# The last image's closing chain: reciprocals spread by products, a convolution started in chunks, depthwise steps shared between two engines, and products that nothing reads

## The chip, the cores and the metric

The kernel runs on one core of a Trainium2 chip. Its time is the device time of one execution in microseconds (us); three executions took 3289.28, 3290.07 and 3290.38 us. The engines are called PE (matrix products), DVE (vector), ACT (activations), POOL and SP (here mostly the queue that starts transfers). All tensors are 32-bit floats.

## The reference, cut to what matters

Eight images x of 512 channels and 64x64 pixels pass two layers, each with a residual connection and a group normalisation of 32 groups in front. The first is a deformable attention with 8 heads; the second is a narrow bottleneck.

```python
x = x + attention(group_norm(x))      # ends: softmax(q k) v, divided by the sum of exps, then w_out
x = x + bottleneck(group_norm(x))

def bottleneck(x):
    y = conv1x1(x, conv_w, conv_b)            # 512 channels to 32, all 4096 pixels
    y = depthwise_conv(y, dw_w, dw_b)         # 3x3, stride 2: 64x64 to 32x32
    y = fc1(y); y = fc2(y)                    # 1024 to 256 to 1024, per channel
    y = depthwise_deconv(y, de_w, de_b)       # 3x3: 32x32 to 64x64
    return conv1x1(y, out_w, out_b)           # 32 channels to 512
```

The group normalisation of the second layer needs mean and variance over all pixels of an image. So the bottleneck of an image can't begin its scaling before the attention of that image has ended.

## The kernel before, in words

The pixels of an image are cut into 8 tiles of 512 (`NT`, `TP`), the channels into 4 blocks of 128 (`NCC`, `P`). Heads go in pairs, so a round of the main loop is one (image, tile, pair of heads), 32 rounds to an image and 256 in all. The order is written out by hand; each engine works through its list in that order. In a round:

- `logits` makes the products of queries and keys and their exponentials for the next round, and `weighted_values` the products with the values (`pa`).
- `sum_exps` adds up the exponentials by products with a selecting matrix into `pn`. After the fourth pair of a tile `invert` takes the reciprocal `rn` on DVE and moves two rows of it to each other half by four small transfers on SP. `scale_two` then spreads one row over 32 partitions (`stream_shuffle`) and multiplies it onto the pair's result, one pair at a time.
- `project_out`, six rounds later (`LAG`), makes one block of `w_out` times the result: eight products of 64 columns each into `pp`. DVE adds bias and residual, and takes statistics (`bn_stats`). The residual itself was read from memory by `load_residual`, over the place that the tile's queries had held.

The bottleneck of image b is `layer1`, a generator. For seven images its pieces lie between the rounds of the next image. For the last image there is no next image: the loop runs `LAG` rounds more without logits, and then `layer1_last` is drained in one go. Its steps, each waiting for the one before: `group_stats` (aggregates on DVE, a product for the group means, small operations on DVE, a product for the variances, a power of -1/2 on POOL); the scaled weights `cw`; the convolution `py`, 32 products of 32 columns; its copy into `y` on ACT, the bias, and three copies of rows that border on another part; nine depthwise steps on DVE into `z`; two transposes `pz` and a copy; the two matrices of the perceptron (`ph`, `pht`, `pu`) with copies between; the deconvolution (`upsample`, four calls for row halves h and parities a, nine DVE operations per h); and `project_last`, 32 products of 32 rows (`out_product`), each evicted with the residual added by DVE (24 of them), or by ACT and then POOL (8 of them, tiles 4 and 5), and each written to memory by a transfer of 256 KB on SP. Transfers on SP stand in the order of the code, so one that isn't ready holds those behind it.

The PSUM pools `ps_s` (two pairs of banks), `ps_a` (`pa` and `pn`) and `ps_mm` (two banks) are shared by all these products. `wflat` is one buffer that holds `y`, `z`, its transpose, `u` and the result `v` of the deconvolution.

Of the kernel before, what the change touches and what calls it, by code (L numbers as in the profile page):

```python
# [49 lines left out]
def kernel(  # L50
# [53 lines left out]
    def q_tile(b, t):  # L104
        return spot(b, t)
# [555 lines left out]
    def project_out(b, t, oc, st):  # L661

        ao, xt = q_tile(b, t), out_tile(b, t)
        pp = ps_mm.tile([P, TP], F32, tag="mm", name=f"pp_{b}_{t}_{oc}")
        for hp in range(NCC):
            for r in (0, DH):
                nc.tensor.matmul(  # L667
                    pp[r : r + DH, :],
                    wout[:, hp, oc * P + r : oc * P + r + DH],
                    ao[:, hp, :],  # L670
                    start=(hp == 0),
                    stop=(hp == NCC - 1),
                )
        nc.vector.scalar_tensor_tensor(  # L674
            xt[:, oc, :], pp, col(V_BOUT + oc), xt[:, oc, :], ALU.add, ALU.add
        )
        nc.vector.bn_stats(st[:, oc, t, :], xt[:, oc, :])  # L677
# [50 lines left out]


    def layer1(b, st, project, place, v):  # L730
# [10 lines left out]
        gs = yield from group_stats(st, 1, b)  # L741
        cw = small.tile([P, NCC, CB], F32, tag="cw", name=f"cw_{b}")
        nc.vector.tensor_mul(cw, convw, gs[:, 1].unsqueeze(2).to_broadcast([P, NCC, CB]))
        yield None

        py = [ps_mm.tile([P, TP], F32, tag="mm", name=f"py_{b}_{h}") for h in range(2)]
        for h in range(2):
            for cc in range(NCC):
                for rb in range(4):
                    nc.tensor.matmul(  # L750
                        py[h][rb * CB : (rb + 1) * CB, :],
                        cw[:, cc, :],
                        out_tile(b, 2 * rb + h)[:, cc, :],
                        start=(cc == 0),
                        stop=(cc == NCC - 1),
                    )

        y = wflat[:, : (ROWS + 1) * (HW + 1)].rearrange("p (r c) -> p r c", c=HW + 1)
        nc.vector.memset(y[:, :, 0:1], 0.0)
        nc.vector.memset(y[0:CB, 0:1, :], 0.0)  # L760
        for h in range(2):
            nc.scalar.copy(
                y[:, 1 + 8 * h : 9 + 8 * h, 1:], py[h].rearrange("p (r c) -> p r c", c=HW)
            )
        pb = ps_mm.tile([P, TP], F32, tag="mm", name=f"pb_{b}")
        for cc in range(NCC):
            for rb in range(4):
                nc.tensor.matmul(
                    pb[rb * CB : (rb + 1) * CB, 0:1],
                    cw[:, cc, :],  # L770
                    gs[:, 0, cc : cc + 1],
                    start=(cc == 0),
                    stop=(cc == NCC - 1),
                )
        yb = small.tile([P, 1], F32, tag="yb", name=f"yb_{b}")
        nc.vector.tensor_sub(yb, col(V_CONVB), pb[:, 0:1])
        nc.vector.tensor_scalar_add(y[:, 1:, 1:], y[:, 1:, 1:], yb)
# [11 lines left out]
        z3 = z.rearrange("p (i j) -> p i j", j=32)  # L789
        for k in range(9):  # L790
            ki, kj = divmod(k, 3)
            yk = y[:, ki : ki + 15 : 2, kj : kj + 63 : 2]
            w = col(V_DWW + k)
            if k == 0:
                nc.vector.tensor_scalar(z3, yk, w, col(V_DWB), ALU.mult, ALU.add)
            else:
                nc.vector.scalar_tensor_tensor(z3, yk, w, z3, ALU.mult, ALU.add)
# [4 lines left out]
        for h in range(2):  # L802
            nc.tensor.transpose(pz[:, h * P : (h + 1) * P], z[:, h * P : (h + 1) * P], ident)
        o += NK
# [6 lines left out]
        for k in range(8):  # L811
            rb, h = divmod(k, 2)
            j = k % 4
            nc.tensor.matmul(
                ph[j * CB : (j + 1) * CB, : 2 * P],
                zT[:, h, rb * CB : (rb + 1) * CB],
                w1[:, k, :],
                start=(k < 4),
                stop=(k >= 4),
            )  # L820
        parts4 = z
# [5 lines left out]
        for oc in range(2):  # L827
# [6 lines left out]
            )  # L834
        hT = small.tile([P, 2, CB], F32, tag="hT", name=f"hT_{b}")
# [8 lines left out]
        for n0, n, rbs in ((0, NK, 4), (NK, 32, 3)):  # L844
            for oc in range(2):
                for rb in range(rbs):
# [7 lines left out]
                    )  # L854

# [28 lines left out]

        for h, a in ((0, 0), (0, 1), (1, 0)):
            upsample(h, a)
            yield None
# [100 lines left out]
    def layer1_last(b, st, other):  # L988
        return layer1(b, st, project_last(other), spot(other, 0), wbuf[:, 0:2, :])
# [69 lines left out]
    with tc.manual_schedule():  # L1059
# [38 lines left out]
        for g in range(len(names) + LAG):  # L1098
# [12 lines left out]
            summed = g % 2 == 0 and 0 <= g - 1 < len(names)  # L1111
            if g % 2 == 0:
                scale_two()
            if g < len(names):
                weighted_values(*names[g])
            if summed:
                sum_exps(*names[g - 1])
            if g < len(names):
                add_exps(*names[g])
# [24 lines left out]
            if 0 <= k < len(names) and k % NCC < 2:  # L1144
                load_residual(*names[k + k % NCC], 2)
# [11 lines left out]
        drain(layer1_last(B - 1, st1s.pop(B - 1), B - 2))  # L1157
# [118 lines left out]
```

## Time and profile before

| | |
|---|---|
| median of the three runs | 3290.07 us (3289.28 to 3290.38) |
| profiled execution, own time | 3290.23 us |
| its span in the profile | 3288.5 us |
| PE busy over the span | 3207.7 us, 98% |
| DVE, ACT, POOL busy | 2330.8, 1186.2, 612.2 us |
| granted PE clock, mean | 0.99 of full speed |
| moved by transfers | 390.62 MB |

The profiled execution lasted 1.7 us longer than its span. The span is cut into 40 slices of 82 us in the page's second part. PE is busy in tenths at 9 in all slices but the first and the last, and the last slice shows PE at 6, the granted clock at 6, and transfers at 125 GB/s. That slice is the closing chain of the last image, and a finer look at it is the way to read this case. A matrix product's entry counts its two passes as two instructions; its end is modelled, so neighbouring products overlap by some hundredths of a microsecond.

### The profile page before, as it was taken

Reading aid. Unit: us, or ns where it says so; the run is one execution under the profiler, and the core shown is the slowest. Engines: PE = TensorE matmul, PEld = TensorE weight load, DVE = VectorE, ACT = ScalarE, POOL = GpSimd, SP = SyncE. Lnnn points to the kernel's source line nnn. Section 1 sums busy time; section 2 is a strip of 40 time slices with the busy share of each in tenths; the row PEclk is TensorE's granted clock in tenths of the full one; section 3 lists DMA queues with packets and bytes.
Section 4 is the critical chain, followed back from the end, with each engine's and each line's share of the span. In section 5 each row is a group of like instructions: output and inputs, shape, how many; then the busy total and the mean of one; then the engine's idle time right before and its main releaser. Section 6 shows DMA issues by size and latency. Waiting matters only on the chain.

```text
span 3288.5 us, 46198 instructions
## 1 busy us (share of the span) xinstructions
PE 3207.7 (98%) x18196; PEld 1531.2 (47%) x18196; DVE 2330.8 (71%) x3786; ACT 1186.2 (36%) x1641; POOL 612.2 (19%) x576
## 2 busy tenths in 40 slices
PE   6999999999999999999999999999999999999996
PEld 5884223348332583326733276332853338433222
DVE  7884765787757777587765977668776687757564
ACT  2343333343333433344333443324433344333520
POOL 1130300130402304022030221303021040310201
PEclk9999999999999999999999999999999999999996
DMA  7232222672327623284333843248232482322713
GB/s 275 77 93 76 76 78 65 198 156 75 113 91 213 126 86 103 78 235 115 104 100 103 209 100 111 83 160 194 71 104 89 181 180 65 121 73 77 130 44 125
DMA packets 293874, 390.62 MB, mean 119 GB/s; under 512 B 18320, under 2 KB 157840, under 8 KB 293648
## 3 DMA queue, kind: packets, MB, share of 16 engines
q1 hardware_dynamic: 240368, 261.72, 24.4%
q0 software_dynamic: 53280, 125.86, 17.1%
q8 instruction: 145, 2.38, 0.3%
q14 instruction: 81, 0.66, 0.1%
HBM read 193.52 MB, written 192.94 MB: 118 GB/s over the span
## 4 chain that ended last, share of the span: by engine, by line
PE 94%; DVE 4%; issue 1%; ACT 0%; DMA 0%; SPq 0%; POOL 0%; ACTq 0%; DVEq 0%; POOLq 0%
PE pp L667 27%; PE pq L275 23%; PE ps L580 14%; PE pa L598 13%; PE pn L625 4%; PE pqt L324 4%; PE pk L533 2%; PE py L750 2%; PE pv L560 2%; PE po L893 2%; DVE rn L638 1%; PE po L424 0%; PE pu L848 0%; DVE st L201 0%; PE po_s L893 0%
## 5 line engine op out<-in xcount | busy, mean ns | idle before, releaser
L667 PE MATMUL pp<-image,wout 128*64 128x512 f32 x3584 | 821.3, 600 | 3.6 <-DVE image L653 3.4
L588 ACT ACTIVATE es<-ps 128x1024 f32<-128x1024 f32 x512 | 504.0, 1022 | 274.0 <-PE ps L580 211.1
L667 PEld LDWEIGHTS pp<-image,wout 128*64 128x64 f32 x3584 | 237.3, 137 | 549.5 <-issue 474.6
L598 PE MATMUL pa<-es,vt 128*64 128x512 f32 x2048 | 488.9, 598 | 1.7 <-ACT es L588 1.7
L275 PE MATMUL pq<-image,wbuf 128*128 128x256 f32 x2048 | 476.3, 381 | 3.3 <-DVE image L217 1.9
L519 POOL DMA_INDIRECT g<-qd,row x256 | 280.4, 1095 | 1056.2 <-DVE row L516 990.0
L580 PE MATMUL ps<-image,kt 64*64 64x512 f32 x3584 | 437.3, 602 | 0.3
L275 PEld LDWEIGHTS pq<-image,wbuf 128*128 128x128 f32 x2048 | 381.8, 191 | 56.0 <-issue 5.0
L674 DVE SCALAR_TENSOR_TENSOR image<-pp,vec,image 128x512 f32<-128x512 f32 x224 | 167.2, 746 | 337.8 <-PE pp L667 334.2
L605 ACT COPY image<-pa 128x512 f32<-128x512 f32 x224 | 131.9, 589 | 658.9 <-PE pa L598 650.5
L610 DVE TENSOR_TENSOR es<-es,es 128x1024 f32<-128x1024 f32 x256 | 310.9, 1215 | 71.4 <-PE pa L598 71.4
L598 PEld LDWEIGHTS pa<-es,vt 128*64 128x64 f32 x2048 | 137.3, 137 | 294.5 <-issue 274.1
L580 PEld LDWEIGHTS ps<-image,kt 64*64 64x64 f32 x3584 | 114.4, 132 | 307.4 <-issue 182.0
L638 DVE RECIPROCAL rn<-pn 128x512 f32<-128x512 f32 x64 | 214.6, 3353 | 7.7 <-PE pn L625 5.8
L334 ACT COPY qr<-pqt 128x512 f32<-128x512 f32 x224 | 131.0, 585 | 238.7 <-PE pqt L324 223.8
L185 POOL TENSOR_TENSOR gs<-ve,nhalf 128x4 f32<-128x4 f32 x16 | 16.6, 1040 | 1022.5 <-DVE ve L184 1022.5
L651 DVE STREAM_SHUFFLE rb<-rn 128x512 f32<-128x512 f32 x256 | 187.4, 732 | 0.1
L275 PE MATMUL pq<-es,es 128*128 128x256 f32 x768 | 181.5, 379 | 0.0
L945 POOL DMA_DIRECT2D out_dram<-part x126 | 138.1, 1324 | 153.9 <-ACT part L940 146.6
L201 DVE BATCH_NORM_STATS2 st<-image 128x6 f32<-128x512 f32 x256 | 159.2, 678 | 7.5 <-DMA image<-in_x_dram 7.4
L677 DVE BATCH_NORM_STATS2 st<-image 128x6 f32<-128x512 f32 x224 | 155.6, 695 | 7.7
L653 DVE TENSOR_TENSOR image<-image,rb 128x512 f32<-128x512 f32 x224 | 155.2, 693 | 7.8
(197 smaller groups left out, 3491.6 us busy)
## 6 DMA issues: line engine op xcount, KB each, us to landing
qd<-qr SPq DMA_DIRECT2D x256, 256.0 KB
image<-in_x_dram SPq DMA_DIRECT2D x112, 512.0 KB
out_dram<-image SPq DMA_DIRECT2D x49, 1024.0 KB
image<-in_x_dram POOLq DMA_DIRECT2D x48, 1024.0 KB
out_dram<-part POOLq DMA_DIRECT2D x126, 256.0 KB
image<-in_x_dram SPq DMA_DIRECT2D x16, 1024.0 KB
wbuf<-in_w_kvT_dram SPq DMA_DIRECT2D x14, 1024.0 KB
out_dram<-spare POOLq DMA_DIRECT2D x56, 256.0 KB
```

The costliest lines, as they stand in the source:

```text
L201: nc.vector.bn_stats(st[:, cc, t, :], x_tile(b, t)[:, cc, :])
L275: nc.tensor.matmul(bank[:, o * 2 * P : (o + 1) * 2 * P], w[:, k, o * P : (o + 1) * P], xh[:, k, :], start=(k == 0), stop=(k == 1),)
L519: nc.gpsimd.indirect_dma_start(held[-1][:, i, :, :].rearrange("p j d -> p (j d)"), None, qd[:, :], bass.IndirectOffsetOnAxis(ap=row[:, ky, ...
L580: nc.tensor.matmul(ps[k : k + DH, a, :], kt[r : r + DH, hp, kc * P + k : kc * P + k + DH], qt[r : r + DH, hp, :], start=True, stop=True,)
L588: nc.scalar.activation(e, ps, AF.Exp)
L598: nc.tensor.matmul(pa[a * DH : (a + 1) * DH, :], vt[:, kc, hd * DH : (hd + 1) * DH], es[kc][:, a, :], start=(kc == 0), stop=(kc == 1),)
L610: nc.vector.tensor_add(es[0], es[0], es[1])
L638: nc.vector.reciprocal(rn, denominators.pop((b, t)))
L651: nc.vector.stream_shuffle(rb, rn, [2 * (hp % 2) + hp // 2] * 32)
L667: nc.tensor.matmul(pp[r : r + DH, :], wout[:, hp, oc * P + r : oc * P + r + DH], ao[:, hp, :], start=(hp == 0), stop=(hp == NCC - 1),)
L674: nc.vector.scalar_tensor_tensor(xt[:, oc, :], pp, col(V_BOUT + oc), xt[:, oc, :], ALU.add, ALU.add)
L677: nc.vector.bn_stats(st[:, oc, t, :], xt[:, oc, :])
```

## The change

The main loop now ends with its last round. What the six rounds more had done is written out behind it for the last tile, and `layer1` gets two new arguments: `conv`, which runs the last tile's projection and the convolution together (`last_tile`), and `diag`, ten diagonal matrices for depthwise taps as products. The other seven images take the old path in the same order.

- Reciprocals: no transfers and no shuffles. Eight products with a column of the identity, broadcast to 64 columns, spread the rows of `rn` into `rb` in PSUM, and DVE multiplies from there.
- Convolution by chunks: mean and scale are worked out per block of 128 channels, inside the projection of the following blocks (`between`), and the convolution takes a block as soon as its scale is there. The bias `yb` is added in the copies of `py`, one half on ACT and one on DVE.
- Depthwise steps shared: taps 5 to 8 of the convolution, and the odd rows of the deconvolution, become products with diagonal matrices. ACT makes the matrices out of the identity and writes the odd rows.
- `keep_up` issues products of 128x512 into a bank that nothing reads, eight in all: one behind the convolution, two behind the depthwise products, one each behind `pz`, `ph` and `pht`, two behind `pu`.

```diff
+    def keep_up(out, n):
+        for _ in range(n):
+            nc.tensor.matmul(out, ident, wout[:, 0, :], start=True, stop=True)
...
+    def last_tile(b, st):
+        t, nm = NT - 1, f"last_{b}"
...
+        def mean(cc):
+            c = slice(cc, cc + 1)
+            nc.vector.bn_aggr(mv[:, cc, :], st[:, cc].rearrange("p t s -> p (t s)"))
+            nc.tensor.matmul(gps[0][:, c], group, mv[:, cc, 0:1], start=True, stop=True)
+            nc.vector.tensor_copy(gs[:, 0, c], gps[0][:, c])
+            nc.vector.tensor_sub(dv[:, c], mv[:, cc, 0:1], gs[:, 0, c])
+            nc.vector.tensor_mul(dv[:, c], dv[:, c], dv[:, c])
+            nc.vector.tensor_add(dv[:, c], dv[:, c], mv[:, cc, 1:2])
+
+        def scale(cc):
+            c = slice(cc, cc + 1)
+            nc.tensor.matmul(gps[1][:, c], group, dv[:, c], start=True, stop=True)
+            nc.vector.tensor_scalar_add(ve[:, c], gps[1][:, c], EPS)
+            nc.gpsimd.tensor_tensor(gs[:, 1, c], ve[:, c], nhalf[:, c], ALU.pow)
+            nc.vector.tensor_scalar(cw[:, cc, :], convw[:, cc, :], gs[:, 1, c], None, ALU.mult)
+
+        def between(oc):
+            def step(hp):
+                if hp == 2 and oc >= 1:
+                    mean(oc - 1)
+                    if oc >= 2:
+                        scale(oc - 2)
+            return step
+
+        for oc in range(NCC):
+            project_out(b, t, oc, st, between(oc))
+        py = ps_s.tile([P, 2, TP], F32, tag="s", name=f"py_{nm}")
+        two = ps_s.tile([P, 2, TP], F32, tag="s", name=f"pb_{nm}")
+        pb, idle = two[:, 0, 0:1], two[:, 1, :]
+        convolve(b, py[:, 0, :], cw, 0, 0)
+        scale(2)
+        convolve(b, py[:, 1, :], cw, 1, 0)
+        convolve(b, py[:, 0, :], cw, 0, 1)
+        mean(3)
+        convolve(b, py[:, 1, :], cw, 1, 1)
+        scale(3)
+        for cc in range(NCC - 1):
+            convolve_mean(pb, cw, gs, cc)
+        for h in range(2):
+            convolve(b, py[:, h, :], cw, h, 2)
+        convolve_mean(pb, cw, gs, 3)
+        for h in range(2):
+            convolve(b, py[:, h, :], cw, h, 3)
...
+        if conv:
+            nc.vector.memset(y[:, :, 0:1], 0.0)
+            nc.vector.memset(y[0:CB, 0:1, :], 0.0)
+            py, pb, idle = conv()
+            keep_up(idle, 1)
+            nc.vector.tensor_sub(yb, col(V_CONVB), pb)
+            for h in range(2):
+                to, fr = y[:, 1 + 8 * h : 9 + 8 * h, 1:], py[h].rearrange("p (r c) -> p r c", c=HW)
+                if h:
+                    nc.vector.tensor_scalar_add(to, fr, yb)
+                else:
+                    nc.scalar.activation(to, fr, AF.Identity, bias=yb)
...
+            if diag and k > 4:
+                nc.tensor.matmul(pd, diag[V_DWW + k], yk, start=(k == 5), stop=(k == 8))
+                if k == 8:
+                    nc.vector.tensor_add(z, z, pd)
+                    keep_up(idle, 2)
...
+        if diag:
+            keep_up(idle, 1)      
...
+        if diag:
+            for h, tag in enumerate(("pa", "pn")):
+                upsample(h, 0)
+                pv = ps_a.tile([P, TP], F32, tag=tag, name=f"pv_{b}_{h}")[:, : 2 * P]
+                rows = pv.rearrange("p (r c) -> p r c", c=HW)
...
+                        nc.tensor.matmul(
+                            rows[:, :, c::2],
+                            diag[V_DEW + k],
+                            u[:, 4 * h + dr : 4 * h + dr + 4, dc : dc + 32],
...
+                nc.scalar.activation(
+                    v[:, h, :].rearrange("p (r c) -> p r c", c=HW)[:, 1::2, :],
+                    rows,
+                    AF.Identity,
+                    bias=col(V_DEB),
+                )
...
-        for g in range(len(names) + LAG):
+        for g in range(len(names)):
...
-        drain(layer1_last(B - 1, st1s.pop(B - 1), B - 2))
+        b, t, st = B - 1, NT - 1, st1s.pop(B - 1)
+        sum_exps(*names[-1])
+        rn = small.tile([P, TP], F32, tag="rn", name="rn_last")
+        nc.vector.reciprocal(rn, denominators.pop((b, t)))
+        diag = {}
+        for i, w in enumerate([V_DWW + k for k in range(5, 9)] + [V_DEW + k for k in (0, 1, 2, 6, 7, 8)]):
+            diag[w] = es4[i // 8][:, i // 4 % 2, i % 4 * P : (i % 4 + 1) * P]
+            nc.scalar.activation(diag[w], ident, AF.Copy, scale=col(w))
+        project_out(b, t - 1, 2, st)
+        rb = [ps_s.tile([P, 2, TP], F32, tag="s", name=f"rb_last_{i}") for i in range(2)]
+        for hp in range(NCC):
+            for a in range(2):
+                row = CB * (2 * a + hp % 2) + hp // 2
+                nc.tensor.matmul(
+                    rb[hp // 2][a * DH : (a + 1) * DH, hp % 2, :],
+                    ident[:, row : row + 1].to_broadcast([P, DH]),
+                    rn,
+                    start=True,
+                    stop=True,
+                )
+        for hp in range(NCC):
+            ao = q_tile(b, t)[:, hp, :]
+            nc.vector.tensor_mul(ao, ao, rb[hp // 2][:, hp % 2, :])
+        project_out(b, t - 1, 3, st)
+        for oc in (0, 2):
+            load_residual(b, t, oc, 2)
+        drain(layer1_last(b, st, b - 1, lambda: last_tile(b, st), diag))
```

## The prediction, made before the changed kernel ran

> **What bounds the kernel now.** I read the page's clock row first, then the closing 100 us in stretches of 4 us, then the chain of waits there, then SP's queue. Up to 3189 us PE is busy without a break and the change moves nothing there, so only the closing chain counts. First the page's head:
>
> ```profile
> span 3288.5 us, 46198 instructions
> PE 3207.7 (98%) x18196; PEld 1531.2 (47%) x18196; DVE 2330.8 (71%) x3786; ACT 1186.2 (36%) x1641; POOL 612.2 (19%) x576
> ```
>
> and stretches of the end; columns are stretch, length, busy time of PE, PEld, DVE, ACT and POOL with instruction counts, granted clock, transfer share, GB/s:
>
> ```profile
> 3201.39:3204.80 3.41, 1.32 (x6) 0.42 (x8) 3.15 (x7) 0.00 (x0) 0.00 (x0) 1.00 0.93 299
> 3204.80:3208.21 3.41, 2.43 (x6) 0.30 (x4) 3.19 (x8) 0.00 (x0) 0.00 (x0) 0.50 0.96 301
> 3235.52:3238.93 3.41, 1.81 (x48) 0.72 (x40) 1.28 (x4) 0.59 (x1) 0.00 (x0) 1.00 0.00 0
> ...
> 3248.00:3252.00 4.00, 2.75 (x31) 1.56 (x31) 1.35 (x6) 0.00 (x0) 0.00 (x0) 0.50 0.00 0
> 3252.00:3256.00 4.00, 0.79 (x4) 0.51 (x8) 3.75 (x14) 0.00 (x0) 0.00 (x0) 0.50 0.00 0
> 3260.00:3264.00 4.00, 4.00 (x14) 2.01 (x14) 3.07 (x6) 1.25 (x2) 1.27 (x1) 0.50 1.00 374
> 3280.00:3284.00 4.00, 0.00 (x0) 0.00 (x0) 0.00 (x0) 0.00 (x0) 0.00 (x0) 0.50 0.81 288
> ```
>
> To be seen: PE idles, its clock falls to half after a stretch that was 39% busy (1.32 of 3.41) and stays full after one that was 53% busy (1.81); from 3260 on the transfers are full. Next the chain, start, length, what:
>
> ```profile
> 3194.48 3.34 DVE rn L638
> ...
> 3199.71 1.69 DMA rn<-rn
> ...
> 3207.32 14.39 PE pp L667 x56
> ...
> 3226.52 1.04 POOL gs L185
> ...
> 3227.93 9.18 PE py L750 x64
> ...
> 3243.90 0.66 PE pz L803 x2
> ```
>
> SP's queue in the timeline, with the first output transfers,
>
> ```profile
> 3258.94 10.71 SPq L983 DMA_DIRECT2D out_dram<-image  x16
> ```
>
> and DVE's last steps before the outputs, start, length, instruction:
>
> ```profile
> 3257.00 1.13 DVE L883 SCALAR_TENSOR_TENSOR wbuf<-wbuf,vec 128x128 f32<-128x128 f32 x3
> 3258.16 2.07 DVE L980 SCALAR_TENSOR_TENSOR image<-po_s,vec,image 128x512 f32<-128x512 f32 x3
> ```
>
> So the time is: end of the rounds, a serial chain up to the first output transfer (3258.94), then 8.39 MB of output at 374 to 382 GB/s, about 22 us, and 4 us behind it. What the change is worth is how much earlier that first transfer is issued. Transfers run until 3284.7, 25.8 us after it.
>
> **The change, part by part.** I put the new order of each engine on before's clock, from 3193.96, where block 2 of tile 6 starts.
>
> *Reciprocals.* Gone: four transfers (SP 2.42, landing 1.69 us) and four shuffles of 0.73. PE's holes behind them (2.10, 0.33, 0.98 us) and the half clock they caused go too. Added: eight products shaped like a block of `pp`; a block costs 3.51 (two took 7.09, of which 0.07 is drain). `rn` ends at 3197.82, so they run 3197.9 to 3201.4. DVE's four multiplications (0.69 each) wait for four products at a time and end at 3203.0, while block 3 runs to 3204.9. Tile 7 then starts warm and without a hole. Its residual moves behind block 3 on SP: issue at 3203.4 instead of 3200.3, landing near 3207.2 (1.1 us to the first bytes, 0.5 MB at 300 GB/s, 1 us to close), before its first use at 3208.5. The 2 MB of weights behind it land 3 to 4 us later, by 3216, needed after 3238. ACT's ten diagonal matrices, by its copies of 128x256 (0.37) and activation of 128x32 (0.20) some 0.28 each, lie in the 43 us in which it did nothing.
>
> *Convolution by chunks.* Four blocks of 3.51 from 3204.9, plus three means and two scales between, 0.36 each (row `gps`): 1.8. The added wait: POOL's power takes 1.04 per block, four times instead of once, and DVE stands behind it each time, with the eviction and statistics of the next block queued behind. So mean 2 is 0.3 late and the projection ends at 3221.1, not 3221.7. No group chain follows; convolution starts at once, not at 3227.93. Block of four products 0.86 (32 of them took 3.43 per 16 when warm). Block 3's mean stands on DVE behind two evictions' work and the power of block 2: PE waits for it from 3224.1 to 3225.75. The convolution ends at 3231.4, not 3237.1: 5.7 gained.
>
> *Bias and copies.* The program orders `yb` behind the first `keep_up`, since both write one PSUM tile, and the DVE half behind the ACT half. So 0.86 + 0.17 + 0.15, then 0.69 on ACT (row L977), 0.7 on DVE, 0.6 for three row copies: 3234.65. Before, 0.60 + 0.77 + 0.6 led to 3239.16. Gained: 4.5.
>
> *Depthwise.* DVE 0.44 + 4 x 0.52 + one addition 0.43 instead of 0.44 + 8 x 0.52: `z` is complete at 3237.65, not 3243.8. PE meanwhile makes four products (two passes of 256 columns, 0.43) and two `keep_up` (0.86), 3234.1 to 3237.6. Gained: 6.2.
>
> *Perceptron.* Warm prices, from the images in the middle: `pht` 0.56 for 1.06 now, `pu` 1.12 for 2.14, `ph` 0.86 for 1.93, `pz` 0.24 for 0.66. Each `keep_up` that outlasts the copy beside it delays the next product: 0.15 before `ph`, 0.2 before `pht`, 0.45 before `pu`, 0.65 before `pv`. `u` is there at 3244.1, PE free at 3244.75. With the first one (0.86), `keep_up` costs 2.3 us on the path.
>
> *Deconvolution.* Twelve products of 128 columns. The nearest row is the transposes `pqt`, 0.117 per pass: 0.23 a product, 2.8 for both halves, to 3247.55; DVE's six even-row steps end at 3246.1 beside it. First products warm 0.85, eviction 0.75: first transfer issued at 3249.25. Before, DVE's upsampling held it until 3258.94. Gained: 9.7.
>
> *Output.* Still the transfers. SP had a hole from 3262.04 to 3263.81, waiting for POOL's second addition, which waited for ACT and for PE at half clock; warm it goes, 0.3 to 1.2 us of transfer time. I take 0.3, since the outputs may run cold again.
>
> Sum: 9.7 + 0.3 = 10.0 us off the profiled 3290.23 (span 3288.5 to 3278.5). The median of the runs is 0.16 below: 3280.0.
>
> [...] The row first: after 39% busy the clock fell, though PE's longest rest was 2.10 us. [...] By the row, each leaves a window about 50% busy in the worst phase, thin single-column products included, just beside 39% and 53%: a drop lasts two windows (3201.39's did: 0.50 until 3211.6) and costs up to 3.4 us, near 3 after rests. The row is this case's own; that is my second case.
>
> The other: no row shows a product that writes every second column of PSUM, as `pv` does. [...] Below, `pqt`'s pace; above, I estimate double: 2.8 us more. I take the row, and keep 2.8 in the range.
>
> **Rivals.**
> 1. *The clock falls once.* For it: the windows above; against: few phases hit it. Gain 7.0: 3283.0.
> 2. *Strided PSUM writes at half pace.* Gain 7.2: 3282.8.
> 3. *Slower: the useless products set the pace.* If the clock stays at half from the end of the convolution, all that PE does there doubles, 15.3 us to about 30: `keep_up` 1.7 each, `pd` 3.5, `pz` to `pu` 5.9, `pv` 5.6. The first transfer comes near 3264.2, 5.3 later than before: 3295.4. It decides once over two thirds of that stretch run cold. For it: in before PE was at half from 3242.35 to 3273, even while listed as wholly busy with 32-row products. Against: these are 128-row products, and convolution brought the clock back in 4 us.
> 4. *Nothing gained at the end*: outputs would have to start no earlier, or take longer. Against: transfers at 0 GB/s right up to 3258. About 3288.
>
> **How the numbers follow.** Case as worked out 0.62 (3277.5 to 3282.5); rival 1 0.16; rival 2 0.12; rival 3 0.06; rival 4 0.04. A measurement here can tell about 0.2%, 6.6 us, so "faster" means below 3283.5. Main case whole, 0.6 of each of rivals 1 and 2: 0.79. Same: the rest of these and rival 4, 0.15. Slower: 0.06. Range 3276.8 (0.9 more from the output's hole, the rest from handovers) to 3285.5 (rivals 1 and 2 with 2.5 on top; both together give 3285.8).
>
> **What would show it.** Right: no `rn` transfers and no PE rest between 3198 and 3221; projection of tile 7 ending near 3221; convolution over near 3231.4 with one rest of 1.7; clock 1.00 up to the outputs; first output issue near 3249.3; transfers full for 22 to 23 us. Wrong: clock 0.50 somewhere in 3225 to 3247 (rivals 1, 3), `pv` above 1.4 per half (rival 2), holes in the output's transfers, or a landing of the residual later than 3208.5, which would hold mean 0.

## The result

Six executions of the changed kernel took 3276.55 to 3278.78 us, median 3277.29, against a median of 3289.68 for six of the kernel before: ratio 0.9964 with a 95% interval of 0.9954 to 0.9974, so 12.4 us less, where 10.0 were predicted. The profiled execution took 3278.49 us (span 3276.7), at the upper end of the six, and is 11.7 us below the profiled one of the kernel before.

### The profile page after: what moved, and what is told of

Same layout as the page of the kernel before. It is cut to its first block, busy times and chain, and to the rows that moved or that the text cites. A ratio compares the mean times of both kernels' runs of the same rounds, so it can differ in the third digit from the quotient of the medians.

```text
span 3276.7 us, 46349 instructions
## 1 busy us (share of the span) xinstructions
PE 3216.0 (98%) x18272; PEld 1538.6 (47%) x18272; DVE 2325.4 (71%) x3781; ACT 1188.8 (36%) x1652; POOL 614.5 (19%) x579
## 4 chain that ended last, share of the span: by engine, by line
PE 95%; DVE 3%; issue 1%; ACT 0%; DMA 0%; SPq 0%; POOL 0%; ACTq 0%; DVEq 0%; POOLq 0%
PE pp L667 27%; PE pq L275 23%; PE ps L580 14%; PE pa L598 13%; PE pn L625 4%; PE pqt L324 4%; PE po L1019 2%; PE pk L533 2%; PE pv L560 2%; PE py L738 1%; DVE rn L638 1%; PE po L424 0%; PE po_s L1019 0%; PE pu L944 0%; PE pf L493 0%
```

## The profile after

The page's head of the changed kernel:

```profile
span 3276.7 us, 46349 instructions
PE 3216.0 (98%) x18272; PEld 1538.6 (47%) x18272; DVE 2325.4 (71%) x3781; ACT 1188.8 (36%) x1652; POOL 614.5 (19%) x579
```

PE is busy 8 us longer than before, in a span that is 11.8 us shorter: its products cover time in which it stood. The chain of waits through the closing part (start, length, engine, tile, line):

```profile
3194.24 3.35 DVE rn_last L1285
3197.64 3.65 PE rb_last L1296 x16
3201.29 9.44 PE pp L667 x44
...
3227.25 1.75 PE py_last L738 x16
3229.00 1.07 PE pb_last L734 x2
3230.09 0.17 DVE yb L834
3230.28 0.70 ACT wbuf L840
3231.00 0.77 DVE wbuf L838
...
3231.81 3.65 PE pd L880 x8
3235.46 1.75 PE pb_last L734 x4
3237.21 0.22 PE pz L893 x2
...
3244.68 2.68 PE pv L996 x24
```

L734 is the product that nothing reads. It stands on the chain twice in these rows (and four times more up to `pv`): ahead of the bias `yb`, which was written down beforehand, and between `pd` and `pz`. And `pd` took 3.65 us; pv_contig, below, shows it at full clock with 2.13. The stretches there and in the outputs show why (stretch, length, busy time of PE, PEld, DVE, ACT and POOL with instruction counts, granted clock, transfer share, GB/s; the first two are windows of the clock record):

```profile
3228.58:3231.99 3.41, 1.65 (x7) 0.48 (x4) 1.09 (x3) 0.69 (x1) 0.00 (x0) 1.00 0.00 0
3231.99:3235.41 3.42, 3.42 (x9) 2.67 (x10) 2.74 (x7) 0.00 (x0) 0.00 (x0) 0.50 0.00 0
3236.00:3240.00 4.00, 4.00 (x25) 1.64 (x24) 0.43 (x1) 0.37 (x1) 0.00 (x0) 1.00 0.00 0
3252.00:3256.00 4.00, 4.00 (x15) 1.80 (x14) 3.80 (x6) 0.69 (x1) 2.41 (x2) 0.56 1.02 381
3268.00:3272.00 4.00, 0.00 (x0) 0.00 (x0) 0.00 (x0) 0.00 (x0) 0.00 (x0) 0.50 1.02 367
```

PE was busy for 1.65 of 3.41 us, 48%, and the clock was at half for the next window, once, and back at full after it. From 3252 to 3272 the transfers are full without a gap. SP's queue and POOL's power in the timeline (start, length, engine and line, operands; in brackets the idle time before it and what ended it):

```profile
3249.25 9.96 SPq L1109 DMA_DIRECT2D out_dram<-image  x16
3215.94 0.57 POOL L781 TENSOR_TENSOR gs_last<-ve_last,nhalf 128x1 f32<-128x1 f32 x1 [116.04 <-DVE ve_last L780]
3225.45 0.54 POOL L781 TENSOR_TENSOR gs_last<-ve_last,nhalf 128x1 f32<-128x1 f32 x1 [2.57 <-DVE ve_last L780]
```

The first output transfer is issued at 3249.25, to the hundredth what was predicted. That is partly chance, as the three parts of the closing stretch show. In the table they are measured from marks of each kernel's own trace: the start of the last reciprocal (`rn`), the end of the convolution, the issue of the first output transfer, the end of the span. The start of `rn` itself lies anywhere between 3193.0 and 3195.0, so a comparison by clock times alone would mix in 2 us of the rounds before. The times come from four batches of runs; the medians of the kernel before lay between 3288.84 and 3289.68 us in them, so times of different batches can be compared to about 1 us.

| kernel (below) | rn at | rn to end of convolution | to first output | to end of span | median of runs (lowest to highest) |
|---|---|---|---|---|---|
| before | 3194.48 | 42.63 | 21.83 | 29.56 | 3289.68 (3288.31 to 3290.38) |
| changed | 3194.24 | 34.76 | 20.25 | 27.45 | 3277.29 (3276.55 to 3278.78) |
| after_again | 3195.02 | 34.76 | 20.27 | 27.55 | 3276.98 (3275.83 to 3279.33) |
| old_recip | 3193.68 | 37.62 | 20.25 | 27.35 | 3280.59 (3279.86 to 3282.96) |
| no_chunks | 3194.44 | 39.54 | 17.41 | 27.81 | 3281.21 (3279.30 to 3281.90) |
| no_diag | 3194.34 | 34.76 | 24.32 | 28.48 | 3283.50 (3281.66 to 3284.17) |
| no_keep | 3194.48 | 34.81 | 19.56 | 27.75 | 3278.15 (3276.47 to 3278.38) |
| before_keep | 3194.13 | 42.99 | 21.29 | 27.99 | 3288.02 (3285.09 to 3289.91) |
| pv_contig | 3193.26 | 34.75 | 18.77 | 28.22 | 3276.75 (one run) |
| fill | 3192.95 | 34.76 | 18.76 | 28.23 | 3277.67 (3276.42 to 3278.16) |
| split | 3194.90 | 34.75 | 17.24 | 28.41 | 3275.88 (3275.07 to 3277.13) |
| split_no_keep | 3193.29 | 34.80 | 18.92 | 27.89 | 3277.33 (3276.41 to 3279.11) |
| sized | 3193.64 | 34.77 | 15.57 | 28.02 | 3273.73 (3273.56 to 3275.10) |
| sized2 | 3194.17 | 34.80 | 15.33 | 27.80 | 3274.08 (3273.44 to 3274.37) |

The 11.8 us between the two spans are 0.24 + 7.87 + 1.58 + 2.11: two thirds of it lie ahead of the end of the convolution, and what follows up to the first output (the bias, the new depthwise steps, the shorter perceptron and the deconvolution) brought 1.58 in this trace.

## The experiments

The theory after reading both traces: the reciprocals and the chunks bring what they should or more; behind the convolution the unread products both hold the clock and stand in the way, and the clock falls there by the phase of its windows; in the outputs, the kernel before lost time because PE began them at half clock. The rival: the unread products and the moved depthwise steps do what the prediction says, and the differences come from the transfers at the end.

**The changed kernel again** (after_again, no edit).

> The changed kernel once more, nothing edited; its trace shows what varies from execution to execution. My theory: every mark up to the end of the convolution comes back within 0.1 us (convolution ends near 3229.0), and what varies is only where the windows of the granted clock (3.41 us long, running free of the program) fall on the thin stretch from 3229 to 3237. If one falls as in the first trace, the clock reads 0.5 once there, the depthwise products take 3.65 us and the first output transfer is issued near 3249.2; if none does, they take 1.75 and it is issued 0.6 to 1.8 us earlier, and the run is near 3276.6. Rival: the fall of the clock is fixed to the program (the same every time), and the runs' spread of 2.2 us comes from the transfers at the end; then the mark is 3249.2 again, and the output phase, 27.45 us from first issue to the end of the span, is what differs.

Its rounds ended 0.78 us later; from there the marks of the two traces agree to 0.02 us up to the first output transfer, the fall of the clock included (`pd` took 3.44 us instead of 3.65, the two products behind it 0.23 more). The stretches of the clock's windows:

```profile
3229.60:3233.02 3.42, 1.66 (x8) 0.69 (x5) 1.33 (x5) 0.69 (x1) 0.00 (x0) 1.00 0.00 0
3233.02:3236.43 3.41, 3.41 (x9) 2.46 (x8) 2.87 (x7) 0.00 (x0) 0.00 (x0) 0.50 0.00 0
```

Two equal falls could be phase or program. Over all eleven executions of this kernel the mean clock of the core splits them: the four with 0.995 took 3278.35 to 3279.33 us, the seven with 0.996 to 0.998 took 3275.83 to 3277.29. The split fits a fall that happens in some executions only. It is not proof, since the clock in the outputs falls in some traces and not in others; the trace of pv_contig, below, shows the other branch.

**Old reciprocals** (old_recip).

```diff
-        rn = small.tile([P, TP], F32, tag="rn", name="rn_last")
-        nc.vector.reciprocal(rn, denominators.pop((b, t)))
+        invert(*names[-1])
...
-        rb = [ps_s.tile([P, 2, TP], F32, tag="s", name=f"rb_last_{i}") for i in range(2)]
...
+        scale_two()
         project_out(b, t - 1, 3, st)
+        scale_two()
```

> Only the reciprocals of the last tile are as before: four small transfers and four shuffles on DVE instead of eight products on PE; all else as changed. My theory: they are worth what the holes and the half clock cost, less the eight products: PE's holes 2.10 + 0.33 + 0.98 and 3.4 us lost in two windows at half clock make 6.8, the products 3.5, and some of DVE's new steps fit into the holes: projection of tile 7 ends 1.5 to 3 us later than 3220.2, clock at 0.5 for two windows near 3205 to 3211, all later marks move by the same; time 3279 to 3280.5. Rival 1: nothing, since the means between the blocks wait for DVE and not for PE: within 0.5 us of the changed kernel. Rival 2: the shuffles (4 of 0.73) put the means and scales late on DVE as well, and the loss is above 4 us: 3281.5 or more.

The end of the convolution moved by 2.86 us (37.62 against 34.76), inside the 1.5 to 3 expected, and the clock stood at 0.5 from 3203.74 to 3210.57, two windows, as in the kernel before. The parts behind it did not move (20.25, 27.35). In time it is 3280.59, 0.1 above what was expected, against 3276.98, and the two ranges do not touch. Both rivals, nothing and more than 4, are out.

**Old statistics and convolution** (no_chunks).

```diff
-        drain(layer1_last(b, st, b - 1, lambda: last_tile(b, st), diag))
+        for oc in range(NCC):
+            project_out(b, t, oc, st)
+        drain(layer1_last(b, st, b - 1, None, diag))
...
+            if diag:
+                idle = ps_s.tile([P, 2, TP], F32, tag="s", name="idle")[:, 1, :]
+                keep_up(idle, 1)
```

> Only the statistics and the convolution of the last tile are as before: four blocks of projection without steps between, then the group chain on DVE and POOL, then the convolution in one piece; the rest as changed (the bias is taken from another PSUM tile than the unread product writes, as before). My theory: the group chain of 6.2 us comes back between the projection (3220.2, or 3219.5 without the small products) and the convolution (9.2 us), which ends near 3235.0; the depthwise step then begins 2.1 us after it instead of 3.4, since the first half is copied beside the convolution and the bias waits for no product. First output transfer about 4.5 to 5 us later than 3249.2, time 3281 to 3282.5. Rival: the chunks only move the waiting from before the convolution into it and behind it: under 2 us, time 3279 or less.

The convolution ended 4.78 us later after `rn` (39.54), at 3233.98, 1.0 earlier than I had put it. Part of this is the clock: in the group chain PE was busy for 0.38 of 3.42 us, and the clock was at half from 3222.05 to 3228.87, into the convolution. With the 2.86 of the reciprocals it makes 7.64 of the 7.87 us that lie ahead of the end of the convolution. The next part was shorter than in the changed kernel, 17.41 us. Its chain shows why: the copies begin at once, with no unread product ahead of them, and the clock did not fall there (`pd` 2.10 instead of 3.65):

```profile
3224.91 9.07 PE py L738 x64
...
3234.00 0.60 ACT wbuf L854
...
3234.62 0.77 DVE wbuf L864
...
3235.53 2.10 PE pd L883 x8
```

So the chunks are worth 4.8 us, and what follows them in the changed kernel's trace gives 2.8 back: 1.5 is the fall of the clock (pv_contig, below), the rest the bias that waits. So the first transfer came 2.1 us later than 3249.25, not the 4.5 to 5 expected; against pv_contig, whose clock held, it is 3.4 (56.95 after `rn` against 53.52). The time, 3281.21, is inside what was expected.

**Depthwise steps on DVE** (no_diag; the list of diagonal matrices is kept only as the sign for the unread products. The two that stood behind `pd` now follow on PE as soon as the bias is taken).

```diff
+        keep, diag = diag, None
...
-        if diag:
+        if keep:
             keep_up(idle, 1)
```

> Only the depthwise steps go back to DVE: all nine taps before the perceptron, and the whole upsampling; the unread products stay where they are. My theory: the first of the two shares brings next to nothing now (z complete at 3232.42 + 0.44 + 8 x 0.52 = 3237.0, while PE comes to the transposes at 3237.05 in the changed kernel, held by the unread products behind the depthwise ones); the second brings about 2 us (u at 3243.7, eighteen steps of 0.38, eviction 0.75, instead of 5.5 us from u to the first transfer) and keeps PE warm at the outputs: first output transfer 3251 to 3251.5, output phase 1 to 2 us longer, time 3279.5 to 3281.5. Rival, the working of the prediction: both shares count, 1.7 for the depthwise step and 3 for the upsampling: first transfer near 3254, time 3282 or more.

First transfer 4.07 us later than in the changed kernel, time 3283.50: as large as the rival said, but not where it said. `pz` begins 8.16 us after the convolution instead of 8.21, so the first share gave nothing in that trace, as my theory had it. What my theory had not seen is that without `pd` PE has no work there for a whole window of the clock record:

```profile
3232.45:3235.86 3.41, 0.00 (x0) 0.00 (x0) 3.16 (x8) 0.00 (x0) 0.00 (x0) 1.00 0.00 0
3235.86:3239.27 3.41, 2.02 (x4) 0.82 (x4) 1.60 (x4) 0.00 (x0) 0.00 (x0) 0.50 0.00 0
```

The clock falls for two windows, and from `pz` to the end of `u` it takes 9.3 us instead of 6.5. In this pair of traces the moved taps pay by feeding PE, not by freeing DVE. Two things limit that. In the changed kernel `pz` was late because the clock fell at `pd`; in pv_contig, where it held, `pz` begins 6.67 us after the convolution, and the first share gives 1.49. And the two unread products that follow `pd` ran here right behind the bias (from 3230.40), which left PE without work for 4.87 us; placed later they might have held the clock, and no run tried it. The upsampling share was 1.35 us (6.87 from `u` to the first transfer against 5.52).

**No unread products** (no_keep): the body of `keep_up` left out.

> The eight products that nothing reads are left out; the outputs are the same. My theory: they pay, but less than their product time, because they both hold the clock and stand in the way. Without them the bias is 1.1 us earlier and the delays before the transposes, the perceptron's products and the deconvolution (1.2 + 0.35 + 0.5 + 0.5 + 0.8) go, 4.4 us in all; but PE is then about 40% busy from 3229 on, its clock falls and stays at half: depthwise products +1.75 (half of it hidden), transposes +0.2, perceptron +2.4, deconvolution +2.8, about 6.5 on the path; the outputs start cold, and SP's queue has its hole again, 1 to 2 us. First output transfer near 3251.3, time 3280 to 3282. Rival: the products only delay: the clock is 1.0 or the cold costs nothing, first transfer near 3244.9, time near 3273.

Neither. The clock fell to half from 3236.01 to 3246.25, so the products do hold it, and `ph`, `pht`, `pu` and `pv` took 9.71 us instead of 5.16:

```profile
3229.18:3232.60 3.42, 1.82 (x12) 1.43 (x8) 2.40 (x7) 0.69 (x1) 0.00 (x0) 1.00 0.00 0
3232.60:3236.01 3.41, 1.33 (x16) 0.56 (x18) 2.13 (x5) 0.00 (x0) 0.00 (x0) 1.00 0.00 0
3236.01:3239.43 3.42, 2.60 (x24) 1.36 (x20) 0.52 (x4) 0.37 (x1) 0.00 (x0) 0.50 0.00 0
```

And yet the first output transfer was issued 0.69 us sooner after the convolution than in the changed kernel's trace (and 0.79 later than in pv_contig, where the clock held). Of the 6.5 us that I had put for the cold, 4.8 came (0.23 in `pz`, 4.55 in the four others); `pd`, whose share I had half on the path, ran before the fall. What went with the products must then have been 4.8 + 0.69, some 5.5 us: the 4.4 of my count, and about 1 us of the fall of the clock at `pd` in the other trace; this split is argued, not measured. In time, 3278.15 against 3276.98, the ranges overlap: as they stand in the changed kernel, the eight products are worth nothing that these runs can tell.

**Only the unread products, on the kernel before** (before_keep).

```diff
+            idle = ps_s.tile([P, 2, TP], F32, tag="s", name="idle")[:, 1, :]
+            keep_up(idle, 7)
...
+            keep_up(idle, 1)      # behind pz, ph and pht; three behind pu
```

> The kernel before, with unread products of the changed kernel's kind alone: seven behind the convolution (beside DVE's bias, copies and depthwise taps), one each behind the transposes and the perceptron's first two products, three behind the third. Nothing else of the change. My theory: PE's clock holds at 1.0 from the convolution to the first outputs; transposes 0.66 to 0.22, perceptron 5.13 to 2.5, of which the overhang of the unread products takes 1.35 back, so the first output transfer comes 1.7 us before 3258.94; and the output phase (first issue to end of span), 29.56 in the kernel before, falls to 27.5 to 28.2, since SP's hole there was PE's half clock. Time 3285 to 3286.2. Rival 1: the hole is POOL's, not PE's: output phase 29 to 29.6, time 3287 or more. Rival 2: the unread products give nothing on balance in front of the outputs either, as in the run without them: the first transfer is where it was, only the output phase gains, time 3287 to 3288.

The clock held from 3232.31 to 3259.61, and `pz` to `u` fell by 1.44 us (6.72 against 8.16), near the 1.7 expected; the outputs took 27.99, inside the range. But the first transfer came only 0.54 us sooner after the convolution, and the time missed what was expected: 3288.02 is 1.66 below before (3289.68 in this batch), with an interval (ratio 0.9994, 0.9986 to 1.0002) that reaches 1. What was given back is in DVE's upsampling (first row: line L899, its count, then lowest, median and highest duration in ns, first and last start; then POOL's timeline):

```profile
L899 DVE SCALAR_TENSOR_TENSOR wbuf<-wbuf,vec x10: 351/353/1233, 3251.3 to 3257.2; 128x128 f32<-128x128 f32 x10
3255.80 1.26 POOL L994 TENSOR_TENSOR image<-image,image 128x512 f32<-128x512 f32 x1 [28.41 <-ACT image L993]
3258.41 10.44 SPq L999 DMA_DIRECT2D out_dram<-image  x16
```

One of ten equal steps took 1233 ns instead of 353, beginning 0.18 us after POOL's first addition and ending 0.17 after it. With PE warm, ACT evicted its first block while DVE was still upsampling, and the step beside POOL's addition (3255.80 to 3257.06) was 0.88 us longer. This is one pair in one trace, so the cause is read from its times, not tested. In the kernel before, the addition began at 3258.16, when DVE was already evicting out of PSUM: three evictions took 2.07 us from there, as the first three in before_keep did, beside which POOL did nothing (from 3257.63).

**Adjacent columns for the deconvolution** (pv_contig).

```diff
-                rows = pv.rearrange("p (r c) -> p r c", c=HW)
+                rows = pv.rearrange("p (c r w) -> p c r w", c=2, w=32)
...
-                            rows[:, :, c::2],
+                            rows[:, c],
```

> The changed kernel, in which the deconvolution's products write 128 adjacent columns of PSUM instead of every second one; ACT's copy out of PSUM takes the interleaved order instead. The profile is read for the 24 passes of these products, 2.68 us in the changed kernel at a clock of 1.0. My theory: 2.6 to 2.7 again, since 0.112 us per pass of 128 columns is the pace of the transposes that write adjacent columns (0.22 for two); ACT's copy stays at 0.48. Rival: strided writes do slow the products, and adjacent ones take half, 1.4 us; then ACT's copy may grow instead.

2.68 us, the same to the hundredth, and ACT's copy 0.47 in both. Columns two apart cost nothing at this size. This trace gave something else: up to `pv` its program is that of the changed kernel, and here the clock did not fall. The windows that hold the same rest, and the chain:

```profile
3227.43:3230.85 3.42, 1.66 (x11) 0.32 (x3) 0.95 (x3) 0.69 (x1) 0.00 (x0) 1.00 0.00 0
3230.85:3234.26 3.41, 3.41 (x12) 2.15 (x12) 3.10 (x9) 0.00 (x0) 0.00 (x0) 1.00 0.00 0
3230.83 2.13 PE pd L880 x8
3232.96 1.72 PE pb_last L734 x4
3234.68 0.28 PE pz L893 x2
```

1.66 us busy and full clock, where 1.65 to 1.66 brought half in the changed kernel, in its second trace and in old_recip. So after 48% it went both ways, and busy time alone does not say which: this window held 0.58 us of the convolution, the three others 0.18 to 0.42, and whether that decides was not tested. The fall costs 1.5 us (20.25 against 18.77).

**One product more in the rest** (fill).

```diff
             nc.vector.tensor_sub(yb, col(V_CONVB), pb)
+            keep_up(idle, 1)
```

> The changed kernel with one unread product more, put behind the bias, where PE rested 1.76 us before the depthwise products in the two traces of the changed kernel; nothing else. In both, the window of the clock record that held this rest was 49% busy (1.67 of 3.41 us), and the next one ran at 0.5. My theory: with it the rest is 0.9 us, no window is below 70% busy and the clock stays at 1.0 up to the outputs; the depthwise products take 1.75 instead of 3.44 to 3.65, the addition to z no longer waits for them, and the first output transfer comes 1.2 to 1.7 us earlier after the end of the convolution (18.6 to 19.1 us instead of 20.25); time 3275.3 to 3276.3. Rival 1: the clock falls all the same, since something other than the rest brings it down: 20.2 and 3277. Rival 2: it holds, but the two unread products behind the depthwise ones keep the transposes where they were: gain below 0.5 us.

The windows there are 2.93 and 3.26 us busy, the clock stayed at 1.0 until 3264.5, and the first transfer came after 18.76 us, where pv_contig had it:

```profile
3226.96:3230.37 3.41, 2.93 (x12) 0.59 (x4) 0.81 (x2) 0.69 (x1) 0.00 (x0) 1.00 0.00 0
3230.37:3233.78 3.41, 3.26 (x12) 2.18 (x12) 3.07 (x10) 0.00 (x0) 0.00 (x0) 1.00 0.00 0
```

The mark is the expected one; the time, 3277.67, is not lower, 1.4 above what was expected. All five runs have a mean clock of 0.997 or 0.998. If most runs of the changed kernel escape the fall anyway, as their mean clocks suggest, the median had little to gain, and the part behind the first transfer was 0.8 us longer in this trace. So what the fall costs is shown by the mark, and not by the median.

**Other PSUM tiles** (split): the means apart from the tile that the unread products write, and a tile for each half of the convolution.

```diff
-        py = ps_s.tile([P, 2, TP], F32, tag="s", name=f"py_{nm}")
-        two = ps_s.tile([P, 2, TP], F32, tag="s", name=f"pb_{nm}")
-        pb, idle = two[:, 0, 0:1], two[:, 1, :]
+        py = [ps_s.tile([P, 2, TP], F32, tag="s", name=f"py_{nm}_{h}")[:, 0, :] for h in range(2)]
+        pb = ps_mm.tile([P, TP], F32, tag="mm", name=f"pb_{nm}")[:, 0:1]
...
+        idle = ps_a.tile([P, TP], F32, tag="pa", name=f"idle_{nm}")
```

> The changed kernel with other PSUM tiles and nothing else: the means of the convolution apart from the tile that the unread products write, and each half of the convolution in a tile of its own. My theory: the bias no longer waits for an unread product (1.1 us) and DVE's half no longer for ACT's (0.7), so the taps begin 1.8 us earlier after the end of the convolution (1.6 to 1.7 us after it instead of 3.4); PE's rest before the depthwise products shrinks from 1.76 to about 0.2, so the clock doesn't fall there, these products take 1.75 in every phase, and the transposes start near 4.8 us after the convolution instead of 8.05. First transfer 3 to 3.5 us earlier (16.8 to 17.3 us after the convolution's end instead of 20.25), time 3273.5 to 3274.5. Rival: the waits named are not what sets it, another follows in their place (the row copies, the taps on DVE): under 1 us. Rival 2: the clock falls all the same, and 1.8 is all: 3275.3.

First transfer 17.24 us after the convolution, as expected, `pz` after 4.79. The expected time, 3273.5 to 3274.5, was missed by 1.4: the outputs took 28.41 in this trace, the longest of all with a warm start, and it was the slowest of the five runs.

**And no unread products** (split_no_keep): the same tiles, the body of `keep_up` left out.

> The kernel with the other PSUM tiles, and without any unread product. It tells whether these products are worth anything once nothing waits for them: the one with the products cut to the rests had its first transfer 15.57 us after the end of the convolution and took 3273.7. My theory: without them the window that holds the rest behind the depthwise products is near 40% busy, the clock falls there and stays at half for three windows as in the first run without them, and the transposes, the perceptron and the deconvolution take 4 to 5 us longer, against 1 us of overhang that goes: first transfer 18.5 to 19 us after the convolution, time 3276.5 to 3277.5. Rival: the work now follows closely enough to hold the clock by itself: 15.5 us or less, 3273 or less.

18.92 us and 3277.33, both as expected: the window behind `pd` was 1.31 us busy of 3.41 and the clock fell for three windows.

**Products cut to the rests** (sized, which gives `keep_up` a width `f` and has the tiles of split; sized2 takes one product of 256 columns away behind the convolution and behind `pd` each, leaving 512 + 256 and 512; the comments in the diff are added here).

```diff
-            nc.tensor.matmul(out, ident, wout[:, 0, :], start=True, stop=True)
+            nc.tensor.matmul(out[:, :f], ident, wout[:, 0, :f], start=True, stop=True)
...
+            keep_up(idle, 2)            # behind the convolution, was 1
+                    keep_up(idle, 1)    # behind pd, was 2
+                    keep_up(idle, 1, NK)
+            keep_up(idle, 1, NK)        # behind pz, ph, pht, was 512 columns
+            keep_up(idle, 1)            # behind pu, was 2
```

> The same other PSUM tiles, and the unread products cut to the rests beside them: two of 512 columns behind the convolution (was one), one of 512 and one of 256 behind the depthwise products (was two of 512), one of 256 behind the transposes and behind each of the perceptron's first two products (was 512), one of 512 behind the third (was two). My theory: besides what the tiles bring, the delays before the perceptron's products (0.35 + 0.5 + 0.5) and most of that before the deconvolution (0.8) go, while PE stays over half busy and the clock holds: first transfer 15.2 to 15.8 us after the convolution's end, time 3272 to 3273. Rival 1: the thinner filling lets the clock fall in some phase, for 3 to 5 us at half: 3275 to 3277, with a spread of 3 us. Rival 2: the unread products never set the pace, and it equals the kernel with the tiles alone.

> The kernel with the other PSUM tiles and the cut products, cut once more where its trace shows them outlasting the rest: behind the convolution one of 512 and one of 256 columns instead of two of 512 (the depthwise products started 0.4 us after their data), and behind the depthwise products one of 512 alone (the transposes started 0.45 us after z). My theory: first transfer 0.4 to 0.5 us earlier, 15.1 us after the end of the convolution, time 3273.3, which the spread of the runs may hide. Rival: the clock falls in some phase, since more rest is left: some runs at 3275 and more.

The chain of sized:

```profile
3228.41 1.91 PE idle_last L734 x4
3230.32 1.86 PE pd L880 x8
3232.18 1.29 PE idle_last L734 x4
3233.47 0.23 PE pz L894 x2
...
3239.15 2.94 PE pv L997 x24
```

15.57 us to the first transfer, clock 1.0 until 3261.27, and 3273.73 us: 0.9953 of before (0.9939 to 0.9967), and every run below every run of the changed kernel; the mark is inside what was expected, the time 0.7 above it. Against split_no_keep, which differs only in the unread products, they are now worth 3.35 us by the mark and 3.6 in time (sized2, of the same batch as split_no_keep: 3.59 and 3.25). The second cut brought 0.24 by the mark, half of what was expected, and nothing in time (3274.08).

## Why the prediction was right, and where it was not

The direction, the range and the main mechanism came out; several terms did not. The median, 3277.29, is 2.7 below the 3280.0 predicted and just below the main case's 3277.5 to 3282.5. Between the two profiled executions the miss is 1.7 us, all of it in the output term below. That the first transfer came at 3249.25 is luck: two errors cancel. From `rn` to the first transfer 36.92 + 17.85 us were predicted (3194.48, 3231.4, 3249.25), and 34.76 + 20.25 measured: the prediction 2.16 too long, then 2.40 too short; the last 0.24 is the earlier `rn`.

*Reciprocals.* Right: products from 3197.64, PE without a rest to the end of tile 7's projection, at 3220.2. old_recip puts a number to them that the prediction did not give: 2.86 us.

*Convolution by chunks.* The mechanism was right and two terms were too big. POOL's power was taken at 1.04, from the row of four columns; a single column took 0.54 to 0.57. So DVE was not late: the rest of 1.65 us before block 3's mean was 0.03, and the 0.3 before mean 2 did not occur. And the mean and scale products, 0.36 each in the working, cost PE 0.31 and 0.22 within the projection.

*Bias and copies.* 3.25 us predicted, 3.42 measured: the first unread product held the bias for 1.07 instead of 0.86. split shows that the order through one PSUM tile was what to look at: with other tiles DVE's taps begin 1.57 us after the convolution, so 1.85 us of it need not be.

*Depthwise and the useless products.* 2.3 us of `keep_up` on the path were predicted. With the clock at full from the convolution to the outputs (pv_contig), the part behind the convolution is 18.77, so 0.92 more than 17.85. `pz` began 6.67 us after the convolution instead of 6.25 (0.2 of it the two products behind `pd`, which the working had at nothing), the way from there to `pv` took 7.53 instead of 7.10, since the products outlast the work beside them by more than was put, `pv` itself was 0.12 shorter, and from its end to the first issue it was 1.89 instead of 1.70.

*The clock.* Rival 1 happened in the profiled trace, at the place that was named, and was given 0.16; half clock between 3225 and 3247 was one of the prediction's own signs of being wrong. That the new rests (put at 1.65 us before block 3's mean and 1.7 before the depthwise products) would cost nothing was the main case's assumption, and no row of the trace before showed it. The row of 39% was the better guide: after 48% busy the clock fell, three times out of four. It cost 1.5 us, not near 3, because it lasted one window and not two. Its way to the end was not the sum in `z`, which waited 0.57 us for `pd`, but PE's own order: `pd` took 1.52 longer, and the two unread products behind it put `pz` off by all of that (8.21 us after the convolution, 6.67 in pv_contig). The chance was too low: a window of 3.41 us holds the whole rest of 1.76 in almost half of all phases.

*Rivals 2 and 3.* 2.68 us for `pv` and pv_contig's 2.68 refute the first, whose half pace was the author's estimate, with no row behind it. The second, PE cold throughout, did not occur, but no_keep shows its place was well chosen: at half clock those steps do take 4.5 us longer.

*Output.* 0.3 was predicted and 2.11 measured: this is the term that was mis-sized. Of these, 1.19 lie between the first issue and that of the last group of SP's queue (20.18 us before, 18.99 now). The first sixteen transfers took 10.71 us to issue in the kernel before and 10.70 in no_diag, the two that began the outputs at half clock; 9.96 or 9.97 in the eleven other kernels that began them at full clock and still were for 3 us; 10.44 in before_keep, where it fell 1.2 us after the first issue. So a cold start costs 0.75, inside the 0.3 to 1.2 of the working, whose lower end was taken because the outputs "may run cold again". They did, but only 3 us after the first issue, and the sixteen issues took 9.96 all the same. Another 0.44 lie in the groups between; no_diag, as cold, does not show them. The other 0.92 lie in the last group itself, before and now:

```profile
3279.12 3.26 SPq L983 DMA_DIRECT2D out_dram<-image  x3
3268.24 2.34 SPq L1109 DMA_DIRECT2D out_dram<-image  x3
```

From the end of these rows to the end of the span it is 6.12 us in both. Over the fourteen traces the last group took 2.00 to 3.48 us with the same work in it, and the stretch behind it 5.86 to 6.22 (6.76 in no_diag). What makes the last group long was not found: the kernel before happened to have a long one, and this part of the gain is luck.

## What to carry to other kernels

Products that keep the clock up belong into a PSUM tile that nothing waits for, and no longer than the rest they fill: the same idea was worth nothing in this kernel as written, and 3.3 to 3.6 us with tiles and lengths put right. Take a small instruction's price from a row of its own width, and when a step is moved to feed another engine, count what that engine would do without it. Judge such a change by marks within the trace, from the last common point on; the time alone mixes in the start, the clock's phase and the end of the transfers, each of 1 to 2 us here.

## What the hardware showed that was not expected

- In the closing chain, up to the outputs, the clock was at half after windows of 3.41 us in which PE was busy for 0% (the kernel before, no_diag), 11% (the kernel before, no_chunks), 38 and 39% (split_no_keep, no_keep, the kernel before) and, three times out of four, 48%; it stayed at full after 53% (1.81 of 3.41 us in the kernel before, 1.82 of 3.42 in no_keep). Elsewhere the share alone does not tell: near 269 us it fell after 91% (3.12 of 3.41 us, in the kernel before and in the changed one). In the outputs, with their 32-row products, it fell after 81% (2.76 of 3.41 us up to 3252.47 in the changed kernel, and alike in after_again, old_recip and split) and stayed after 81% in no_keep and no_chunks. In the closing chain it was back after one window that was wholly busy with 128-row products (from 3208.21 and 3228.69 in the kernel before, 3231.99 in the changed one); PE listed as wholly busy with 32-row products had it at 0.5 for three windows, from 3253.5 to 3263.74, in after_again. What the clock counts is not shown by these runs.
- A DVE step of 128x128 took 1233 ns instead of 353 beside one POOL addition of 128x512 (1.26 us), once, in before_keep.
- The power on POOL takes 0.55 us for 128x1 and 1.04 for 128x4: its fixed part is some 0.4 us, an estimate by a line through the two.
